# Layer 0 of a two-layer transformer block: values meet exponentials in two steps of a job instead of four

## The chip, the cores and the metric

The kernel runs on one core of one Trainium2 chip. The metric is the device time of one launch in microseconds (us). It was run three times before the change: 2089.46, 2091.49 and 2093.51 us, so the median is 2091.49 us.

The core has five engines with a queue of their own each: PE (matrix products; its weight loads are shown apart, as PEld), DVE (vector), ACT (activation functions), POOL and SP (here SP only issues DMAs). PE writes to PSUM, which this kernel takes as eight banks of 128 partitions by 512 fp32 values. All data is fp32.

## The reference

Eight sequences of 512 tokens with 256 features go through two layers. In each, a normalized input goes into an attention branch and a feed-forward branch, and both are added to the residual. The change is in layer 0:

```python
x = L0_attn_x                                   # (8, 512, 256)
xn = _layernorm(x)
# attention, 16 heads of 16 features, no mask, no scale
qkv = (xn @ W_qkv + b_qkv).reshape(B, D, 3, H, p).transpose(2, 0, 3, 1, 4)
q, k, v = qkv
scores = softmax(einsum('bhip,bhjp->bhij', q, k))
attn = einsum('bhij,bhjp->bhip', scores, v)
# experts: each token goes to the one of 8 experts that its affinity picks
es = argmax(xn @ centroids.T); alpha = sigmoid(max(xn @ centroids.T))
ffn = alpha * (xn + relu(ln(xn) @ w1[es].T + b1[es]) @ w2[es].T + b2[es]) + (1 - alpha) * xn
x = x + attn + ffn
```

Layer 1 then runs two causal attentions with a convolution between them, and a low-rank feed-forward branch. The change does not touch its code.

## The kernel before

**Jobs and steps.** Layer 0's attention is cut into 32 jobs: sequence b (8) by group g of four heads (4). A job is worked in 8 steps for the row maxima (`Job.scores`) and, 12 steps later (`LEAD[0]`), in 8 steps for the exponentials (`Job.exps`). Between the two, `Job.shift` turns the maxima round on PE (L375), copies them (L380, DVE) and puts them by four small DMAs into a spare row of the queries (L382, SP), so that the second product comes out already shifted. `run` (L442) walks over the steps. One step t does the following on PE, in this order:

- the scores: two heads of maxima (L345) and two heads of exponents (L394), four products of 32 rows each that run side by side on the four strips of 32 rows of PE. A step's exponents are of one block of 128 keys (`kc`) and one pair of heads (`SC_SEQ[0]`), so a block of keys is complete after two steps;
- the filling (`work_of.fill`, L488): other work of layer 0 by due times and costs, such as projections (L293), values (L303), the expert branch (`Block`: L785, L807, L828). It comes in pieces, so that some steps get none;
- the attends (`attend`, L489 and L427): for the blocks of keys that `AV_AT[0]` (L85) lists for this step, `Job.attend` multiplies exponentials by values (L434): four heads, each on its own 32 columns of PE, into the one bank of `av`.

DVE follows the scores with two maxima (L362), ACT with two exponentials (L421). In the text, step i of a job means the step with its exponents i = 0 to 7; an attend listed at 8 falls into step 0 of the next job. After the last block, `l0_done` (L901) transposes the result on DVE (L904), divides (L906, L908) and adds on POOL (L912).

**Banks.** The maxima take turns on a ring `mx`, the exponents on a ring `sc`: three banks each (`banks_alone`), but two each while the experts run (`banks_experts`, L218). After the last maxima, `sc` has five (`banks_last`) and one turn of the loop does two steps of exponents.

**Experts.** The normalized tokens are scattered by expert into two DRAM arrays `hs_d` (L749), which were filled with zeros before (L866, two DMAs on SP). Then 23 blocks of 256 tokens follow. `Block(n+1)` is made right after the first quarter of block n's hidden layer: it gathers its weights (`w`, L764, POOL's queue), loads its tokens from both arrays into `hs0` and `hs1` (L773, SP) and adds them on POOL (L778). `features` transposes them on PE (L785) after the last quarter of block n. `output` adds the bias on DVE into `f` (L837) and SP stores `f` (L839). `hs0`, `hs1` and `f` have one buffer each.

**Order.** The kernel writes out the order of every engine's queue itself (`manual_schedule`, L156); the framework only adds semaphores.

## Time and profile before

| What | us |
|---|---|
| median of three runs | 2091.49 |
| profiled execution, its own time | 2091.93 |
| its span on the core | 2090.0 |
| PE busy | 2001.5 (96%) |
| DVE busy | 1230.1 (59%) |
| ACT busy | 867.6 (42%) |
| POOL busy | 203.4 (10%) |

The stages, as the trace lays them out:

| us from the span's start | stage |
|---|---|
| 0 to 70 | norms, first maxima, affinities; zeros go to DRAM from 10.56 on |
| 70 to 180 | attention of layer 0 with routing and scatters, little filling |
| 180 to 928 | attention with the experts as filling |
| 928 to 989 | the last jobs, gathers, second norm |
| 989 to 1112 | layer 1's feed-forward branch |
| 1112 to 2090 | layer 1's attentions |

PE's busy share counts matmuls that are pipelined and whose ends are modelled, so 96% does not mean that nothing is lost. What a piece costs PE is better read from starts: from the first instruction of one group to the first of the next. In the timeline, each line is a run of like instructions: start, duration, engine, line, operation, out<-in, shapes, count, and in brackets the idle time before it with what ended it. An fp32 product shows as two instructions.

### The profile page before, as it was taken

How to read it: one execution, taken by the hardware profiler on the slowest of the kernel's cores; microseconds unless marked ns; L12 is line 12 of the kernel's file. 1: busy time of each engine (PE TensorE's matmuls, PEld its weight loads, DVE VectorE, ACT ScalarE, POOL GpSimd, SP SyncE). 2: the span in 40 equal slices, each digit the busy share in tenths (PEclk: the TensorE clock that was granted, in tenths of full speed). 3: DMA queues.
4: the chain of work that ended last, by engine and by line, in shares of the span. 5: the costliest groups of instructions: out<-in, count | busy, mean ns of one | idle time of the engine just before them, and what ended most of it. 6: DMA issues, size and time to landing. Idle time of an engine off the chain costs nothing.

```text
span 2090.0 us, 35594 instructions
## 1 busy us (share of the span) xinstructions
PE 2001.5 (96%) x13672; PEld 1013.6 (48%) x13672; DVE 1230.1 (59%) x3565; ACT 867.6 (42%) x1690; POOL 203.4 (10%) x245
## 2 busy tenths in 40 slices
PE   5899999999999999998898999999999999999998
PEld 3334555555555555542334455554555555554554
DVE  5765555555455455565425666666666666666763
ACT  4444333333333333346541444444444444444444
POOL 4361010010110100013310000000000000000000
PEclk8899999999999999999997899999999999999999
DMA  9015132222322122202000000000000000000000
GB/s 329 25 64 184 59 117 81 94 79 96 117 78 97 67 108 107 74 26 80 21 0 1 2 2 2 2 12 2 2 13 2 12 2 12 2 12 2 2 12 21
DMA packets 46058, 105.60 MB, mean 51 GB/s; under 512 B 5953, under 2 KB 33985, under 8 KB 42945
## 3 DMA queue, kind: packets, MB, share of 16 engines
q0 software_dynamic: 6384, 59.78, 7.7%
q1 hardware_dynamic: 38656, 42.62, 6.1%
q8 instruction: 107, 1.75, 0.4%
q10 hardware_dynamic: 848, 0.93, 0.1%
q14 instruction: 63, 0.51, 0.1%
HBM read 76.05 MB, written 26.48 MB: 49 GB/s over the span
## 4 chain that ended last, share of the span: by engine, by line
PE 87%; DVE 6%; ACT 2%; issue 2%; DMA 1%; SPq 0%; POOL 0%; ACTq 0%; DVEq 0%; POOLq 0%
PE bank L345 30%; PE bank L434 13%; PE bank L828 8%; PE bank L807 8%; PE bank L293 5%; PE bank L412 4%; PE bank L1085 4%; PE bank L394 3%; PE bank L303 3%; PE bank L1103 2%; DVE m L362 2%; PE bank L990 1%; PE bank L1137 1%; PE bank L266 1%; PE bank L1003 1%
## 5 line engine op out<-in xcount | busy, mean ns | idle before, releaser
L421 ACT ACTIVATE e<-bank 128x512 f32<-128x512 f32 (+1 forms) x1280 | 639.1, 552 | 919.5 <-PE bank L394 460.4
L345 PE MATMUL bank<-k,q 32*128 32x512 f32 (+3 forms) x3072 | 761.0, 534 | 22.2 <-DVE m L362 18.3
L394 PE MATMUL bank<-q,k 32*128 32x512 f32 (+3 forms) x3072 | 681.2, 533 | 4.5 <-DMA q<-mT 3.4
L365 DVE CUSTOM_DVE_ANT_0 jk<-bank,cmask 128x512 bf16<-128x512 f32 (+3 forms) x1024 | 502.9, 491 | 240.8 <-PE bank L345 162.4
L345 PEld LDWEIGHTS bank<-k,q 32*128 32x128 f32 x3072 | 301.2, 186 | 384.1 <-issue 162.1
L362 DVE TENSOR_REDUCE m<-bank 128x1 f32<-128x512 f32 x512 | 328.9, 685 | 142.8 <-PE bank L394 111.8
L434 PE MATMUL bank<-e,v 128*32 128x512 f32 (+3 forms) x3072 | 317.4, 501 | 0.0
L394 PEld LDWEIGHTS bank<-q,k 32*128 32x128 f32 x3072 | 266.2, 186 | 15.0 <-issue 9.6
L807 PE MATMUL bank<-hsT,w 128*128 128x256 f32 x736 | 179.6, 389 | 1.3 <-DVE hsT L790 1.3
L828 PE MATMUL bank<-w,hT 128*128 128x256 f32 x736 | 170.9, 386 | 0.0
L807 PEld LDWEIGHTS bank<-hsT,w 128*128 128x128 f32 x736 | 133.3, 190 | 69.9 <-issue 52.8
L828 PEld LDWEIGHTS bank<-w,hT 128*128 128x128 f32 x736 | 137.4, 191 | 38.1 <-issue 21.0
L434 PEld LDWEIGHTS bank<-e,v 128*32 128x32 f32 x3072 | 67.5, 108 | 137.1 <-issue 132.0
L412 PE MATMUL bank<-mask_t,ident_bf 128*128 128x128 bf16 (+1 forms) x768 | 123.5, 244 | 0.0
L412 PEld LDWEIGHTS <-ident_bf 128*128 128x128 bf16 x768 | 44.0, 97 | 155.5 <-issue 140.5
L820 DVE TENSOR_SCALAR hT<-bank,w 128x256 f32<-128x256 f32 x92 | 44.5, 484 | 110.3 <-ACT hT L818 110.3
L1085 PE MATMUL bank<-ctxT,cw_sb 128*128 128x256 f32 x384 | 90.0, 383 | 2.1 <-DVE q L283 1.8
L365 DVE DVE_READ_ACCUMULATOR2_ANT m<- 128x1 f32 x1024 | 85.0, 83 | 0.0
L837 DVE TENSOR_TENSOR f<-bank,w 128x256 f32<-128x256 f32 x46 | 19.5, 425 | 104.2 <-PE bank L828 104.1
L285 ACT ACTIVATE k<-bank,bqk,rows 128x512 f32<-128x512 f32 x64 | 46.3, 773 | 73.8 <-PE bank L293 64.5
L818 ACT ACTIVATE hT<-bank,w 128x256 f32<-128x256 f32 x92 | 43.6, 474 | 79.8 <-PE bank L807 79.8
L1085 PEld LDWEIGHTS bank<-ctxT,cw_sb 128*128 128x128 f32 x384 | 70.1, 189 | 13.2 <-DVE q L283 3.2
(187 smaller groups left out, 1410.5 us busy)
## 6 DMA issues: line engine op xcount, KB each, us to landing
hs_d<-zeros SPq DMA_DIRECT2D x2, 5888.0 KB
hs<-hs_d SPq DMA_DIRECT2D x46, 256.0 KB
q<-mT SPq DMA_DIRECT2D x384, 2.0 KB
fs_d<-f SPq DMA_DIRECT2D x23, 256.0 KB
acc<-in_x SPq DMA_DIRECT2D x8, 512.0 KB
out<-acc SPq DMA_DIRECT2D x8, 512.0 KB
cw_sb<-in_conv_w SPq DMA_DIRECT2D x1, 768.0 KB
wqk<-in_a_wqk ACTq DMA_DIRECT2D x1, 512.0 KB
```

The costliest lines, as they stand in the source:

```text
L293: nc.tensor.matmul(ps, lhsT=w[:, k, col : col + P], rhs=src[:, k, :], start=(k == 0), stop=(k == 1))
L303: nc.tensor.matmul(ps[:, j * D : (j + 1) * D], lhsT=src[:, k, c * P : (c + 1) * P], rhs=w[:, k, :], start=(k == 0), stop=(k == 1),)
L345: lambda h=h, qc=qc, at=at, nk=nk: nc.tensor.matmul(heads[h % 2][:, at : at + nk], lhsT=self.q[h * PH : (h + 1) * PH, qc * P : (qc + 1) * ...
L362: nc.vector.tensor_reduce(self.m[:, qc, h, :], src, AX.X, ALU.max, negate=True)
L365: nc.vector.tensor_tensor_reduce(out=junk[:, :nk], in0=src, in1=cmask[:, S - nk :], scale=1.0, scalar=-3e38, op0=ALU.add, op1=ALU.max, acc ...
L394: lambda h=h, kc=kc, at=at, lo=lo: nc.tensor.matmul(heads[h % 2][:, at : at + S - lo], lhsT=self.k[h * PH : (h + 1) * PH, kc * P : (kc + 1 ...
L412: nc.tensor.matmul(heads[h][:, : len(blocks) * P], lhsT=ident_bf, rhs=mask_t[:, : len(blocks) * P], start=False, stop=True,)
L421: nc.scalar.activation(e[:, h, :], heads[h][:, :n], AF.Exp, scale=self.scale)
L434: nc.tensor.matmul(self.av[h * PH : (h + 1) * PH, lo:], lhsT=self.v[:, kc, 4 * self.g + h, :], rhs=es[h // 2][:, h % 2, :], start=first, s ...
L807: nc.tensor.matmul(ps[:, i * TB : (i + 1) * TB], lhsT=w[:, O_W1 + k * FF + fc * P : O_W1 + k * FF + (fc + 1) * P], rhs=self.hsT[:, k, :], ...
L828: nc.tensor.matmul(ps[:, 0:D], lhsT=self.hT[:, fc, j * P : (j + 1) * P], rhs=w[:, O_W2 + fc * D : O_W2 + (fc + 1) * D], start=(fc == 0), s ...
L1085: nc.tensor.matmul(ps[:, :w], lhsT=cw_sb[:, k, tap, c * P : (c + 1) * P], rhs=ctxT[b % 2][:, k, tap + lo : tap + lo + w], start=(k == 0 an ...
```

## The change

Layer 0's attends are listed for two steps of a job, two blocks each, instead of for four steps with one block each. Exponentials of up to four steps then wait for their values, so their ring gets a fifth tile (128 partitions of 4 KB). Its memory comes from two places: the tile of zeros is halved (the two DMAs that clear `hs_d` now write rows of 1 KB instead of 2 KB, as many bytes), and `hs1` shares the buffer of `f`.

```diff
 AV_AT = (
-    {2: (0,), 4: (1,), 6: (2,), 8: (3,)}, {5: (0,), 6: (1, 3), 7: (2,)}, {2: (0,), 4: (1, 3), 6: (2,)},
+    {4: (0, 1), 8: (2, 3)}, {5: (0,), 6: (1, 3), 7: (2,)}, {2: (0,), 4: (1, 3), 6: (2,)},
 )
...
                 e = self.pool.tile(
                     [P, 2, n], F32, tag=f"e{blocks[0]}" if self.causal else "e", name=f"e{self.nm}_{i}",
-                    bufs=3 if self.causal else 4,
+                    bufs=3 if self.causal else 5,
                 )
...
-        zeros = pre.tile([P, 2 * D], F32, name="zeros")
+        zeros = pre.tile([P, D], F32, name="zeros")
         nc.gpsimd.memset(zeros, 0.0)
-        hs_z = [h.rearrange("(n p r) d -> p n (r d)", p=P, r=2) for h in hs_d]
+        hs_z = [h.rearrange("(n p) d -> p n d", p=P) for h in hs_d]
...
-                    hs = moe.tile([P, TB // P, D], F32, tag=f"hs{i}", name=f"hs{n}_{i}", bufs=1)
+                    hs = moe.tile([P, TB // P, D], F32, tag=("hs", "f")[i], name=f"hs{n}_{i}", bufs=1)
...
-                        nc.sync.dma_start(out=h, in_=zeros.unsqueeze(1).to_broadcast([P, NBLK, 2 * D]))
+                        nc.sync.dma_start(out=h, in_=zeros.unsqueeze(1).to_broadcast([P, NBLK * TB // P, D]))
```

In the built programs every engine has as many instructions as before. On PE only the attends stand in other places: those listed for 2 and 6 have moved to 4 and 8, behind the same step's filling. The other queues keep their order; what is new there are two waits: each `hs1` load (SP) also waits until an earlier store of `f` has landed, and each first write of `f` (DVE) also waits for POOL's sum of the next block's tokens.

## The prediction

> **What bounds the kernel now.** I read the page first: the busy shares and the shares of the chain of waits by line.

> ```profile
> PE 2001.5 (96%) x13672; PEld 1013.6 (48%) x13672; DVE 1230.1 (59%) x3565; ACT 867.6 (42%) x1690; POOL 203.4 (10%) x245
> PE 87%; DVE 6%; ACT 2%; issue 2%; DMA 1%; SPq 0%; POOL 0%; ACTq 0%; DVEq 0%; POOLq 0%
> ```

> PE sets the end, so the question is what PE gets through, stage by stage. The windows by stage (PE, PEld, DVE, ACT, POOL busy, granted clock, DMA share, GB/s):

> ```profile
> 70.00:180.00 110.00, 99.27 (x537) 34.88 (x536) 73.41 (x144) 47.99 (x88) 57.51 (x72) 0.95 0.29 100
> 180.00:928.00 748.00, 735.37 (x4051) 393.93 (x4050) 391.00 (x706) 266.93 (x496) 65.37 (x67) 1.00 0.24 87
> 928.00:989.00 61.00, 51.64 (x295) 17.22 (x292) 39.18 (x94) 39.26 (x74) 25.69 (x27) 0.94 0.29 86
> ```

> Layer 0 is PE's in the expert stage, less so before and after it. Then PE's timeline, close up. First in the expert stage:

> ```profile
> 883.83 1.07 PE L434 MATMUL bank<-e,v 128*32 128x512 f32 x8
> 884.82 0.70 PE L345 MATMUL bank<-k,q 32*128 32x512 f32 x2
> 884.84 0.70 PE L394 MATMUL bank<-q,k 32*128 32x512 f32 x2
> ...
> 886.73 1.29 PE L345 MATMUL bank<-k,q 32*128 32x512 f32 x3 [0.76 <-DVE m L362]
> 887.33 0.70 PE L394 MATMUL bank<-q,k 32*128 32x512 f32 x2
> ...
> 888.39 1.99 PE L303 MATMUL bank<-wv,xT 128*128 128x256 f32 x8
> 890.32 1.06 PE L434 MATMUL bank<-e,v 128*32 128x512 f32 x8
> 891.31 0.70 PE L345 MATMUL bank<-k,q 32*128 32x512 f32 x2
> ```

> Starts give PE's price list: an attend of one block 0.99 (883.83 to 884.82, 890.32 to 891.31), the scores 1.07 (887.33 to 888.39), eight filling products 1.93. But the step at 884.84 has neither filling nor attend, and the next one's exponents start only at 887.33, 2.49 later: PE waits for DVE's maxima to free the banks. I call a step without filling bare. Then the same stretch before the experts, with three banks a ring:

> ```profile
> 142.15 1.06 PE L434 MATMUL bank<-e,v 128*32 128x512 f32 x8
> 143.16 0.70 PE L394 MATMUL bank<-q,k 32*128 32x512 f32 x2
> 145.06 0.70 PE L394 MATMUL bank<-q,k 32*128 32x512 f32 x2
> 146.12 1.06 PE L434 MATMUL bank<-e,v 128*32 128x512 f32 x8
> ```

> A bare step lasts 1.90 here (143.16 to 145.06), and 2.07 with an attend (1.07 + 0.99).

> **What a merge saves.** Layer 1 shows attends of other widths:

> ```profile
> 1502.33 0.64 PE L434 MATMUL bank<-e,v 128*32 128x256 f32 x8
> 1502.90 0.48 PE L345 MATMUL bank<-k,q 32*128 32x256 f32 x2
> ...
> 1514.58 1.07 PE L434 MATMUL bank<-e,v 128*32 128x384 f32 x16
> 1515.58 0.59 PE L345 MATMUL bank<-k,q 32*128 32x384 f32 x2
> ```

> 256 columns take 0.57; two blocks in one go (384 + 128 columns, 16 instructions) take 1.00, as much as one block of 512. So an attend is 0.143 once plus 0.853 per 512 columns (1.00 = a + b, 0.57 = a + b/2). Two blocks together: 1.85 instead of 1.99. There are 64 merges (32 jobs, two each): 64 x 0.142 = 9.1 us, if PE pays for every attend.

> [...]

> **The sum, step by step.** I listed from PE's timeline, for the steps of layer 0, what stands between one group of L394 and the next. Steps i = 2 and 6 of a job lose an attend, i = 0 and 4 double theirs.

> *Expert stage (steps 40 to 230 of 256).* Losing: 48 steps. 36 have filling and get 0.995 shorter: -35.8. 12 are bare: these last 2.50 with an attend (857.53 to 860.02) as without one (2.49 above), so they save 0. Doubling: 48 steps. 42 have filling: +0.853 each, +35.8. 6 are bare: from 2.50 to 1.07 + 1.85 = 2.92, +0.42 each, +2.5. Sum +2.5. Filling without an attend (1.07 + 1.93 = 3.00) stays above 2.50, so no new wait arises.

> *Two blocks of experts whose tokens come late.*

> ```profile
> 679.20 1.26 POOL L778 TENSOR_TENSOR hs<-hs,hs 128x512 f32<-128x512 f32 x1 [15.62 <-DMA hs<-hs_d]
> 680.52 0.42 PEld L785 LDWEIGHTS bank<-ident,hs 128*128 128x128 f32 x4 [1.62 <-POOL hs L778]
> ```

> PE waits for block 16's tokens; for block 18 POOL's sum ends at 745.57 and PE's transposes start at 745.63. Both loads follow, on SP's queue, a shift in a step 5; the transposes are in the step 7 after it. Step 6 between them loses its attend, PE comes 1.0 earlier and waits as much longer. So 1.0 of the saving is lost twice: +2.0 (0 to 3).

> *Before the experts (steps 4 to 39, nine half jobs).* Nearly all bare. Four steps last 2.07 + 1.90 + 2.07 + 1.90 = 7.94. Afterwards 2.92 + 1.90 + x + y, where x and y are bare steps that follow a bare step; the trace has none with three banks. Lower end 1.20 each: DVE's maxima start 0.60 apart (144.31, 144.91, 145.51), two a step. Upper end 1.90 as now. So 7.22 to 8.62, -0.72 to +0.68 a half job. Between them: ACT's exponential starts 1.24 after its product (143.16 to 144.39) and takes 0.60, so a product that comes 1.20 after the last one finds its second bank free only at 1.90; its strip is then held for 0.86 to 2.76. That makes x 1.20, y 1.56 and some 0.5 carried into the doubled step: 8.08, +0.15. Times nine: +1.4 (-6.5 to +6.1).

> *Steps 232 to 243.* DVE is busy all of 934 to 944 (2.00 of each 2 us), so attends there cost nothing now. Of the doubled ones, the two in a step 0 are covered by `l0_done` on DVE (1.4: 932.47 to 934.01 and its like), the third is not wholly: +0.5 (0 to 2.5).

> *End of layer 0.* PE mostly waits for ACT. The last attend (987.65 to 988.65) becomes double, with layer 1's first product right behind it: +0.85 (0 to 1.7).

> *Fifth tile.* The exponentials of step i + 5 take the tile of step i, which the attend of step i + 4 at the latest has read; on PE this stands before the scores that step i + 5 waits for anyway: 0. The bank `av` has four steps of rest instead of two: 0, as no wait for it shows now.

> *Zeros.* As many bytes in rows half as long. 2 x 5888 KB went at 408 GB/s (25 to 40 us); the loads of `acc`, with rows of 1 KB, at 349 (5 to 15 us). So 34.5 instead of 29.6 us: the end moves from about 47 to 52. Next on SP's queue is the first shift at 64.97, the scatters start at 83.58: hidden, 0. Without that cover it would cost 5.

> *`hs1` in `f`'s buffer.* `hs1` waits for the store of the block before the current one. The nearest row for its landing: POOL's first gather waits for the last store, issued at 926.50, and starts at 929.55, so 3.05 at most. In eleven blocks the store is issued 0.5 before the loads (395.90, 396.36), so `hs1` starts up to 2.1 later. Behind it on SP stand shifts, needed three steps on. POOL's sum ends 6.2 or more before PE's transposes in these eleven. Worst case: the load falls among the weights' 2.2 MB, as for block 1, where POOL's sum starts 12.35 after the weights' issue (169.27 to 181.62). For block 14 that gives 595.12 + 12.35 + 1.27 = 608.74, against transposes at 608.88; blocks 5, 7, 12, 17 are alike. They just make it: 0; if not, about 1 each, +5. DVE's `f` waits for POOL's sum of the next block: 680.47 against 685.93, long done.

> Sum: 2.5 + 2.0 + 1.4 + 0.5 + 0.85 = +7.3. The profiled span of 2090.0 becomes 2097.3; around it lie 1.9 (2091.93 - 2090.0), and that run is 0.4 above the median of the three, so I put it onto the median: 2091.5 + 7.3 = 2098.8.

> **The rivals.**
> - *Every attend is paid (faster).* The merges save their 9.1, and bare steps give room elsewhere: 2082.4. For it: the widths in layer 1, PE at 96%. Against it: the bare steps, which last as long without an attend.
> - *Bare steps in a row run at DVE's pace (no change).* x = y = 1.20 before the experts: 7.3 - 1.4 - 6.5 = -0.6, 2090.9. For it: DVE is 67% busy there (73.41 of 110). Against it: the exponents' banks.
> - *Bare steps keep their 1.90 (slower still).* +6.1 instead of +1.4: 2103.5. It decides as soon as x + y exceeds 3.5. For it: it is the only length the trace shows.

> **How the numbers follow.** Forecast 0.58 (its own range 2094 to 2103), every attend paid 0.12, DVE's pace 0.15, 1.90 kept 0.15. Two tenths of a per cent, about what a measurement can tell, are 4.2 us: below 2087.3 is faster, above 2095.7 slower. Faster: the first rival and a little, 0.13. Same: the second, and the forecast's low end, 0.10, together 0.25. Slower: 0.62. The lows of the parts reach the second rival, the highs, with late `hs1`, 2106; the low end is put to 2086 for a part of the first rival.

> **What would show it.** In the profile after: attends of 16 instructions taking 1.85; bare steps 2 and 6 in the expert stage still 2.50 long; the wait of L785 for POOL longer by 1.0 at blocks 16 and 18; steps 2 and 3 before the experts near 1.2 and 1.6; `hs_d<-zeros` landed before 60 us. The prediction is wrong if bare steps shrink with their attend taken away, if two blocks cost other than 1.85, or if L785 waits in more blocks.

## The result and the profile after

| | before | after |
|---|---|---|
| median (us) | 2089.40 (6 runs, 2088.76 to 2093.51) | 2111.07 (6 runs, 2105.05 to 2113.64) |
| profiled execution, its own time | 2091.93 | 2105.97 |
| its span | 2090.0 | 2104.1 |

The changed kernel is slower: ratio 1.0093, 95% interval 1.008 to 1.0107. Two later sets of runs of it gave 1.0072 and 1.0089. The direction was foreseen. The size was not: +7.3 us was predicted, and the measured time lies above the predicted range. The medians are 21.7 us apart. The profiled execution of the kernel after is one of its two fastest, 5.1 below its median, and shows +14.2 us; so some 7 us of that difference show in no profile of this pair. The stretches of the profiled execution say where the 14.2 are. The marks are the starts of the first exponents (L394) of a step, of L978 and of layer 1's first maxima:

| stretch | before | after | difference | predicted |
|---|---|---|---|---|
| start to step 4 | 86.16 | 83.77 | -2.39 | 0 |
| steps 4 to 39 | 94.41 | 100.51 | +6.10 | +1.4 |
| steps 40 to 230 (experts) | 747.88 | 750.76 | +2.88 | +2.5 + 2.0 |
| steps 231 to 247 | 36.87 | 39.19 | +2.32 | +0.5 |
| step 248 to the first L978 | 23.33 | 26.56 | +3.23 | +0.85 |
| feed-forward of layer 1 | 120.61 | 122.26 | +1.65 | 0 |
| attentions of layer 1 | 980.69 | 981.09 | +0.40 | 0 |

The page of the kernel after, its busy times and the shares of its chain of waits:

```profile
PE 2000.3 (95%) x13672; PEld 1023.9 (49%) x13672; DVE 1230.2 (58%) x3565; ACT 868.3 (41%) x1690; POOL 204.6 (10%) x245
PE 87%; DVE 7%; ACT 3%; issue 2%; DMA 1%; POOL 0%; SPq 0%; ACTq 0%; DVEq 0%; POOLq 0%
```

PE is busy for 1.2 us less than before, and the span is 14 longer, so PE waits longer. It also works more slowly in places, as the windows by stage of the kernel after show (PE, PEld, DVE, ACT, POOL busy, granted clock, DMA share, GB/s). The granted clock is the share of PE's full clock that it was given; 0.50 is half clock.

```profile
70.00:184.00 114.00, 100.81 (x520) 41.42 (x519) 71.24 (x140) 46.87 (x85) 57.69 (x73) 0.93 0.28 98
184.00:935.00 751.00, 727.45 (x4052) 396.06 (x4050) 391.40 (x706) 267.30 (x496) 65.13 (x67) 1.00 0.24 86
935.00:1001.00 66.00, 55.42 (x299) 19.33 (x298) 38.43 (x93) 39.40 (x73) 27.14 (x27) 0.90 0.26 78
```

Against 0.95, 1.00 and 0.94 before, the granted clock is lower in the two stages where time was lost beyond the prediction: before and after the experts. First PE's timeline of the kernel after in the expert stage, to be laid beside the same steps of before:

```profile
891.28 0.70 PE L394 MATMUL bank<-q,k 32*128 32x512 f32 x2
...
893.77 0.70 PE L394 MATMUL bank<-q,k 32*128 32x512 f32 x2
...
894.83 1.99 PE L303 MATMUL bank<-wv,xT 128*128 128x256 f32 x8
896.76 1.92 PE L434 MATMUL bank<-e,v 128*32 128x512 f32 x16
898.61 0.70 PE L345 MATMUL bank<-k,q 32*128 32x512 f32 x2
```

Two blocks in one go take 1.85 (896.76 to 898.61); the bare step still lasts 2.49 (891.28 to 893.77). Then step 4, which has the first doubled attend. Before the change it ran at full clock (1.00 from 86.16 to 94.00):

```profile
86.16 0.70 PE L394 MATMUL bank<-q,k 32*128 32x512 f32 x2
...
87.22 1.07 PE L434 MATMUL bank<-e,v 128*32 128x512 f32 x8
88.22 0.70 PE L345 MATMUL bank<-k,q 32*128 32x512 f32 x2
```

And in the kernel after:

```profile
80.60 0.69 PE L345 MATMUL bank<-k,q 32*128 32x512 f32 x1 [2.23 <-DVE m L362]
...
83.77 1.22 PE L394 MATMUL bank<-q,k 32*128 32x512 f32 x2
...
85.78 3.20 PE L434 MATMUL bank<-e,v 128*32 128x512 f32 x16
88.90 0.70 PE L345 MATMUL bank<-k,q 32*128 32x512 f32 x2
```

A doubled attend, the same 16 instructions as above, takes 3.12 here (85.78 to 88.90) instead of 1.85, and the scores ahead of it 2.01 instead of 1.07. Behind step 38 it is the same with the first experts' products; the first line is of the kernel before, the second of the kernel after:

```profile
175.21 5.42 PE L807 MATMUL bank<-hsT,w 128*128 128x256 f32 x24 [1.27 <-DVE hsT L790]
```

```profile
177.34 7.00 PE L807 MATMUL bank<-hsT,w 128*128 128x256 f32 x24 [1.62 <-DVE hsT L790]
```

The windows around the two places in the kernel after (columns as above):

```profile
78.20:81.60 3.40, 1.17 (x9) 0.52 (x8) 3.23 (x9) 0.60 (x1) 0.42 (x1) 1.00 0.01 2
81.60:88.40 6.80, 6.51 (x27) 1.40 (x23) 3.82 (x8) 2.17 (x4) 6.10 (x8) 0.50 0.18 61
173.70:177.10 3.40, 2.02 (x12) 0.85 (x10) 2.08 (x4) 1.84 (x4) 0.00 (x0) 1.00 1.00 426
177.10:180.50 3.40, 3.16 (x8) 2.56 (x9) 0.59 (x2) 0.00 (x0) 0.00 (x0) 0.51 1.00 422
```

In the 3.4 us before (as long as the shorter of the two stretches at half clock), PE was busy for 1.17 and 2.02, with longest single gaps of 2.23 and 1.62; after that it was granted half its clock (0.50 and 0.51) for 6.8 and 3.4 us. An attend stood in both places before the change (steps 2 and 38). This gave the theory for the experiments: the prediction's prices are right, and what it lacks is that an attend in a place where PE waits anyway is not only free, it also keeps the clock up.

### The profile page after: what moved, and what is told of

It is laid out like the page before. It is cut to its first block, busy times and chain, and to the rows that moved or that the text cites. A ratio compares the mean times of both kernels' runs of the same rounds, so it can differ in the third digit from the quotient of the medians.

```text
span 2104.1 us, 35591 instructions
## 1 busy us (share of the span) xinstructions
PE 2000.3 (95%) x13672; PEld 1023.9 (49%) x13672; DVE 1230.2 (58%) x3565; ACT 868.3 (41%) x1690; POOL 204.6 (10%) x245
## 4 chain that ended last, share of the span: by engine, by line
PE 87%; DVE 7%; ACT 3%; issue 2%; DMA 1%; POOL 0%; SPq 0%; ACTq 0%; DVEq 0%; POOLq 0%
PE bank L345 29%; PE bank L434 13%; PE bank L807 8%; PE bank L828 8%; PE bank L293 5%; PE bank L1085 4%; PE bank L412 4%; PE bank L394 3%; PE bank L303 3%; DVE m L362 2%; PE bank L1103 2%; PE bank L266 1%; PE bank L1137 1%; PE bank L990 1%; PE bank L1003 1%
## 5 line engine op out<-in xcount | busy, mean ns | idle before, releaser
L345 PE MATMUL bank<-k,q 32*128 32x512 f32 (+3 forms) x3072 | 761.8, 533 | 32.4 <-DVE m L362 28.4
L394 PE MATMUL bank<-q,k 32*128 32x512 f32 (+3 forms) x3072 | 688.2, 534 | 4.2 <-DMA q<-mT 3.1
L345 PEld LDWEIGHTS bank<-k,q 32*128 32x128 f32 x3072 | 302.5, 186 | 370.8 <-issue 157.9
L362 DVE TENSOR_REDUCE m<-bank 128x1 f32<-128x512 f32 x512 | 328.8, 685 | 121.3 <-PE bank L394 94.7
L434 PE MATMUL bank<-e,v 128*32 128x512 f32 (+3 forms) x3072 | 305.0, 500 | 0.0
L394 PEld LDWEIGHTS bank<-q,k 32*128 32x128 f32 x3072 | 270.3, 186 | 18.4 <-ACT e L421 8.7
L434 PEld LDWEIGHTS bank<-e,v 128*32 128x32 f32 x3072 | 74.4, 109 | 146.9 <-issue 142.2
```

What stands on the lines that cost most here:

```text
L345: lambda h=h, qc=qc, at=at, nk=nk: nc.tensor.matmul(heads[h % 2][:, at : at + nk], lhsT=self.q[h * PH : (h + 1) * PH, qc * P : (qc + 1) * ...
L362: nc.vector.tensor_reduce(self.m[:, qc, h, :], src, AX.X, ALU.max, negate=True)
L394: lambda h=h, kc=kc, at=at, lo=lo: nc.tensor.matmul(heads[h % 2][:, at : at + S - lo], lhsT=self.k[h * PH : (h + 1) * PH, kc * P : (kc + 1 ...
L434: nc.tensor.matmul(self.av[h * PH : (h + 1) * PH, lo:], lhsT=self.v[:, kc, 4 * self.g + h, :], rhs=es[h // 2][:, h % 2, :], start=first, s ...
```

## The experiments

All of them are compared with runs of the kernel before on the same chip. On the chips of e9/e10 and e11/e12 that kernel itself took 2098.3 and 2102.0, elsewhere 2089.4 to 2091.7, so times of different chips are not set against each other. In the profiles the difference lies mainly in steps 231 to 247: they take 45.73 in e10 and 38.24 in e5, which is the same program, and 49.54 in e12 and 39.19 in the kernel after. Why was not looked into. In kernels with added lines, the same code stands up to five lines further down.

### The memory edits alone (e1)

```diff
 # before, with zeros in rows of 1 KB and hs1 in the buffer of f; four tiles
```

> The kernel before with the change's memory edits alone: zeros in rows of 1 KB, hs1 in f's buffer; four tiles and four attends a job as before. Theory (the loss is what the attends no longer hide, plus lost clock where PE waits longer): 0, within 2 us of before. Rival (the memory edits delay the experts' tokens or the scatters): most of the loss of 15 to 20 us, 2100 or more.

Measured: 2089.61 against 2091.70, ratio 0.9981 (0.9965 to 0.9997). The two edits cost nothing. In the kernel after the longer way of `hs1` shows, but stays hidden: for block 14 POOL's sum runs from 613.44 to 614.71, 10.7 after the weights' issue at 602.72 instead of 3.7 as before, and PE's transposes start at 616.34.

### One merge at a time (e2, e3, e4)

```diff
-    {4: (0, 1), 8: (2, 3)},
+    {4: (0, 1), 6: (2,), 8: (3,)},     # e2
+    {2: (0,), 4: (1,), 8: (2, 3)},     # e3
```

e4 is the kernel after, unchanged, on the same chip.

> The kernel after with attends {4: (0, 1), 6: (2,), 8: (3,)}: one merge a job, the one in step 4. By the list of steps: expert stage 18 filled steps 2 lose 0.995 (-17.9), 6 bare ones lose nothing, 19 filled steps 4 gain 0.853 (+16.2), 5 bare ones 0.42 (+2.1): +0.4; the rest near 0. Theory: +0 to +3 us. Rival (each merge costs the same, or memory costs): +8 to +20.

> The kernel after with attends {2: (0,), 4: (1,), 8: (2, 3)}: one merge a job, the one in the next job's step 0. By the list: expert stage 18 filled steps 6 lose 0.995 (-17.9) of which 2.0 comes back as waits for blocks 16 and 18, 6 bare ones lose nothing, 23 filled steps 0 gain 0.853 (+19.6), one bare one 0.43: +4.1; before the experts +0.7, end of layer 0 +0.85 and 0.5: about +6, and on top whatever clock is lost at the end of layer 0. Theory: +6 to +14 us, nearly all of the change's loss. Rival (each merge costs the same): half of the loss, +8 to +10; if memory costs: +15 or more.

> The kernel after, unchanged, for another profile beside the others. Theory: 2104 to 2113 us; the price of each step the same as in the first profile (step 4 before the experts 3.2, filled steps as listed), and what differs from run to run is where the granted clock is 0.5. Rival (the spread comes from DMAs): steps of the expert stage differ between the profiles.

Measured: e2 2092.48, ratio 1.0008 (0.999 to 1.0025); e3 2102.01, 1.0058 (1.0041 to 1.0076); e4 2107.31, 1.0072 (1.0051 to 1.0093). Step 4 of e4 took 5.12, at half clock again, and not the 3.2 expected. By the times, most of the loss comes with the second merge, which empties steps 6: step 38 and the steps ahead of the two late blocks among them. By the stretches the two are nearer. Steps 4 to 39 take 97.6 in e2 and 97.5 in e3, against 94.4 before and 100.5 after. Each merge has its place there: e2 has the half clock in step 4, behind the empty step 2, and e3 has it in step 39, behind the empty step 38. Steps 40 to 230 take 747.3 and 752.6 (747.9 before), step 231 to the first L978 62.6 and 65.3 (60.2 before). For e2 these sum to +5.0, where its median shows +0.8; its profile has layer 1's attentions 7.8 shorter than that of before. The programs do not differ there, and that stage takes 973 to 982 us in the sixteen profiles; why it varies was not settled.

### Old places at the ends only (e6)

```diff
-            av_at = AV_AT[job.seq]
+            av_at = OLD if layer == 0 and j in (0, 4, 29, 30, 31) else AV_AT[job.seq]
```

`OLD` is the list of before; the other 27 jobs have the merges.

> The kernel after, with attends in four steps again in jobs 0, 4, 29, 30 and 31 alone, that is at the start of the exponentials, ahead of the experts and at the end of layer 0. Theory: these three places make most of what the sum by steps missed; step 4 falls from 5.15 to 2.07, step 39 from 10.73 to about 8.4, the end of layer 0 comes within 1 us of that of before relative to step 231; what is left is the expert stage's +3 to +6: 2094 to 2099 us. Rival (the loss is spread evenly over the merges): 27 of 32 jobs are still merged, so 0.84 of the loss: 2105 or more.

Measured: 2096.02 against 2090.04, ratio 1.0033 (1.0018 to 1.0049). Five jobs of 32 undone take back more than half of the loss: step 231 to the first L978 lasts 60.03 (60.20 before, 65.75 after), step 39 8.39 (8.35 and 10.73).

### What a bare step holds (e5, e7, e9, e10)

e5 is the kernel before, with 14 attends put off by one step, from a filled step into the bare step behind it; four tiles, no merge.

```diff
+LATER = (50, 52, 76, 90, 108, 134, 136, 150, 152, 162, 176, 178, 194, 218)
...
-                attends.setdefault(lead + steps * j + i, []).append(...)
+                at = steps * j + i
+                if layer == 0 and at in LATER:
+                    at += 1
+                attends.setdefault(lead + at, []).append(...)
```

> The kernel before (four tiles, four attends a job, no memory edit) with 14 attends put off by one step, from a filled step of the expert stage into the bare step after it. Theory (an attend in a bare step of that stage is free): the filled steps get 0.99 shorter, the bare ones stay at 2.50: -14 us, about 2077. Rival (PE pays for every attend wherever it stands): 0, within 2 us of before.

Measured: 2074.78 against 2090.04, ratio 0.9933 (0.9913 to 0.9954): faster than both kernels, by about what was expected. PE's timeline of e5, the step that the prediction quoted as bare (884.84 before):

```profile
866.42 0.70 PE L397 MATMUL bank<-q,k 32*128 32x512 f32 x2
...
867.47 1.06 PE L437 MATMUL bank<-e,v 128*32 128x512 f32 x8
868.47 1.13 PE L348 MATMUL bank<-k,q 32*128 32x512 f32 x2
868.91 0.70 PE L397 MATMUL bank<-q,k 32*128 32x512 f32 x2
```

It has an attend now and lasts 2.49, as without one. The 14 steps that gave theirs away are 0.99 to 1.00 shorter each. (Step 178 is 2.68 shorter: the profile of before had a granted clock of 0.50 from 723.10 to 726.50 there.)

e7 is the kernel before with a third bank for the maxima, taken from the filling.

```diff
-        share_banks(mx=banks[:2], sc=banks[4:6], av=banks[6:7], mm=banks[2:4] + banks[7:])
+        share_banks(mx=banks[:3], sc=banks[4:6], av=banks[6:7], mm=banks[3:4] + banks[7:])
```

> The kernel before with three banks for the maxima in the expert stage, and two instead of three for projections, values and experts. Theory (a bare step lasts 2.50 there because two banks wait for DVE's maxima): bare steps fall to 1.9 to 2.1, 32 of them: -10 to -14 us, less what the filling loses by its third bank. Rival (bare steps wait for the exponentials): bare steps stay at 2.4 or more; time 0 or worse.

Measured: 2086.38 against 2090.04, ratio 0.9985 (0.9971 to 0.9998), less than expected. PE's timeline of e7, a step that took 2.50 before (857.53 to 860.02):

```profile
852.65 0.70 PE L394 MATMUL bank<-q,k 32*128 32x512 f32 x2
...
853.71 1.07 PE L434 MATMUL bank<-e,v 128*32 128x512 f32 x8
...
854.72 0.99 PE L394 MATMUL bank<-q,k 32*128 32x512 f32 x2
```

It takes 2.07, the PE work alone. Bare steps without an attend go from 2.50 to 1.90. So the banks of the maxima set the 2.50. All 32 bare steps together are 15.7 shorter than before; the filled ones, with two banks instead of three for the filling, are 10.1 longer, and that is why little is left.

e9 is e5 with a fifth tile (and the memory edits for it) and 7 further attends put off by two steps, into bare steps that have one already. e10 is e5 again, on the same chip.

```diff
+MERGE = (68, 82, 100, 116, 140, 210, 226)
...
+                    at += 1 if at in LATER else 2 if at in MERGE else 0
```

> The kernel before, with the 14 attends of the cover experiment put off by one step into bare steps of the expert stage, and 7 further attends put off by two steps, into a bare step that has one attend already (so that this step has two blocks in a row, as in the change), with the change's memory edits for the fifth tile. My theory (an attend in a bare step is free, two of them make it 2.92 instead of 2.50, and an attend taken out of a filled step saves 0.995): the 14 give what the cover experiment gave (about -15 us against the kernel before), the 7 give 7 x (0.995 - 0.42) = -4 more: -19, about 2071. Rival (PE must not be idle at all: the saving is given back, by a lower granted clock or by later waits): -15 or less, 2075 or more. Second rival (the fifth tile or the waits of the memory edits cost something once the stage is shorter): above 2078.

> The cover experiment once more, on the same chip as the one with 7 merges, for their difference: about 2075. By my theory it stands 4 us above the other, by the rivals level with it or below it.

Measured: e9 2079.83, ratio 0.9917 (0.9893 to 0.994); e10 2082.49, 0.9921 (0.99 to 0.9942). The times alone do not tell the two apart. The profiles do, in the expert stage: against e10 the bare steps are 3.01 longer (7 x 0.43) and the filled ones 6.86 shorter (7 x 0.98), together -3.9 where -4 was expected. So merging pays where the attend leaves a filled step for a bare one.

### Unread work in the idle places (e8, e11, e12)

e8 is the kernel after with one product behind steps 2 and 38, which nothing reads.

```diff
+            if layer == 0 and t - lead in (2, 38):
+                nc.tensor.matmul(bank(), lhsT=ident, rhs=xT[0][:, 0, :], start=True, stop=True)
             attend(t)
```

> The kernel after, with one product of 128 rows by 512 columns that nobody reads added behind steps 2 and 38, where an attend was taken away: work is added, nothing moved. Theory (there PE idles so long without the attend that the granted clock is 0.5 in the steps that follow): the clock stays or returns to 1.0, step 4 falls from 5.15 to 3.2 and step 39 from 10.7 to about 8.5: 3 to 5 us faster than after. Rival (the steps are long for another reason): 0 to 2 us slower than after.

Measured: 2104.21 against 2090.04, ratio 1.0075 (1.0055 to 1.0096). That is not apart from e4's 1.0072 on the same chip; the time alone decides nothing. PE's timeline of e8, step 4 and the first experts' products:

```profile
84.77 0.70 PE L394 MATMUL bank<-q,k 32*128 32x512 f32 x2
...
85.83 1.93 PE L434 MATMUL bank<-e,v 128*32 128x512 f32 x16
87.68 0.70 PE L345 MATMUL bank<-k,q 32*128 32x512 f32 x2
...
176.34 5.42 PE L809 MATMUL bank<-hsT,w 128*128 128x256 f32 x24 [1.32 <-DVE hsT L792]
```

Step 4 takes 2.92 instead of 5.15, step 39 8.39 instead of 10.73: 4.6 us that were half clock and nothing else, since the instructions of these steps are the same (granted 1.00 from 177.10 to 180.50 in e8, 0.51 in the kernel after). Not all of it is a gain: step 40 starts 2.6 us earlier than in the kernel after (181.70 instead of 184.28), as the start of step 4 is 1.0 later and step 38 is 0.8 longer.

All sixteen profiles (before, after and the fourteen runs) agree. In four of them (after, e2, e4, e12) step 2 has nothing but its scores, and in these four step 4 has 4.6 to 5.1 us of half clock; in the twelve others it has none. In four (after, e3, e4, e12) step 38 has nothing but its scores, and in these four step 39 has 3.4 us of half clock; in the twelve others it has none.

e11 was meant to do this at the end of layer 0 too, with two more products ahead of the transposes of sequences 5 and 7. e12 is the kernel after, on the same chip.

```diff
         ps = bank()
+        if nm in ("c5", "c7") and k == 0:
+            for _ in range(2):
+                nc.tensor.matmul(ps, lhsT=ident, rhs=xT1[0][:, 0, :], start=True, stop=True)
```

> The kernel after, with one unread product of 512 columns behind steps 2 and 38, and two such products ahead of the transposes (L266) of the tokens of sequences 5 and 7 at the end of layer 0, where PE otherwise waits 2.3 us for ACT's normalized tokens; nothing reads the products. Theory of the granted clock (PE idle for a few us, then half the clock for 3.4 or 6.8 us, in which a doubled attend takes 2.6 instead of 1.9): the windows at half clock from 983 on are gone, the attends and scores behind them are back at 1.92 and 1.14, and the stretch from step 231 to the first L978 is 3 us shorter than the 65.7 of the kernel after; with the 2.6 at step 39 the whole is 5 to 7 us faster than the kernel after. Rival (only the cover that the attends gave to the wait for ACT is lost, the clock does not matter): 65 to 67 us as before, the whole at most 3 us faster than after.

> The kernel after, unchanged, on the same chip as the one with four places filled by unread products, for their difference: 1.007 to 1.011 of the kernel before; 65 to 67 us from step 231 to the first L978.

Measured: e11 2116.45, ratio 1.0063 (1.0047 to 1.0079); e12 2121.27, 1.0089 (1.0073 to 1.0104). The products missed their place: sequences 5 and 7 are transposed in layer 1, where they ran at 1069 and 1093. So e11 tells nothing of layer 0's end; it is e8 once more, and beside e12 it is 4.8 us faster. From step 231 to the first L978 e12 took 75.5 us, not the 65 to 67 expected; this is where its chip is slower.

### The end of layer 0 (e13, e14)

e13 has the two pairs ahead of the transposes of sequences 1 and 3, e14 is e8 again on the same chip.

```diff
-        if nm in ("c5", "c7") and k == 0:
+        if nm in ("c1", "c3") and k == 0:
```

> The kernel after, with one unread product of 512 columns behind steps 2 and 38, and two such products ahead of the transposes (L266) of the tokens of sequences 1 and 3, where PE otherwise waits 2.3 us for ACT's normalized tokens at the end of layer 0; nothing reads the products. Theory of the granted clock: the windows at half clock that fall on the last two attends are gone, these attends are back from 2.6 to 1.92 and the scores ahead of them from 2.09 to 1.14, and the stretch from the last wait for the shifted queries to the first L978 is 2 to 3 us shorter than in the kernel without the pairs on the same chip. Rival (only cover is lost, ACT sets the pace): the attends stay at 2.6 or the stretch stays within 0.5 us.

> The kernel after, with one unread product behind steps 2 and 38 only, on the same chip as the one with two pairs more: 3 to 5 us faster than the kernel after (1.005 to 1.008 of the kernel before); half clock on one or two of the last three attends (2.6 instead of 1.92).

Measured: e13 2097.94 against 2090.25, ratio 1.0043 (1.0028 to 1.0059); e14 2104.81, 1.0075 (1.0051 to 1.0099). By the medians the unread work in two more places saves 6.9 us; the profiles show how much of this is its doing. PE's timeline of e14, without the pairs:

```profile
981.54 1.81 PE L266 MATMUL bank<-ident,yn 128*128 128x128 f32 x6 [2.28 <-ACT yn L257]
983.29 2.09 PE L394 MATMUL bank<-q,k 32*128 32x512 f32 x8
985.31 2.82 PE L434 MATMUL bank<-e,v 128*32 128x512 f32 x16
...
995.58 2.81 PE L434 MATMUL bank<-e,v 128*32 128x512 f32 x16
998.32 1.98 PE L980 MATMUL bank<-yT,u_sb 128*128 128x512 f32 x4
```

And of e13, with them (L267 is the unread work):

```profile
978.91 1.99 PE L267 MATMUL bank<-yT,ident 128*128 128x512 f32 x4 [0.35 <-DVE yT L271]
...
982.87 1.14 PE L397 MATMUL bank<-q,k 32*128 32x512 f32 x8
983.94 1.92 PE L437 MATMUL bank<-e,v 128*32 128x512 f32 x16
...
992.78 1.92 PE L437 MATMUL bank<-e,v 128*32 128x512 f32 x16
994.64 1.98 PE L983 MATMUL bank<-yT,u_sb 128*128 128x512 f32 x4
```

The wait of 2.28 is filled, the attends take 1.92 instead of 2.8, the scores 1.14 instead of 2.09. The granted clock says the same; the first window is e14's, the second e13's:

```profile
980.40:987.20 6.80, 5.64 (x26) 2.21 (x30) 0.69 (x1) 4.22 (x9) 0.00 (x0) 0.50 0.00 0
```

```profile
980.30:987.10 6.80, 5.53 (x37) 2.01 (x35) 0.69 (x1) 6.34 (x14) 0.00 (x0) 1.00 0.00 0
```

From step 248 to the first L978 it is 23.02 instead of 26.84. This is 3.8 of the 7.6 us between the two spans. Another 3.6 lies in layer 1's attentions (977.45 and 981.10), where the programs do not differ; that stage takes 973 to 982 in the profiles, longest where a stretch of 20.5 us at half clock falls at its start instead of 6.8 us, and is not counted for the pairs.

## Why the prediction was right in direction and wrong in size

*Expert stage, +2.5, and late blocks, +2.0: right.* Bare steps that lost their attend stayed at 2.50, filled ones became 1.00 shorter, doubled ones 0.86 longer, bare doubled ones 2.92. Step 167 (4.87 to 5.76) and step 183 (5.26 to 6.33) gave the saving back to the tokens of blocks 16 and 18; the kernel after, PE's weight load ahead of its first transpose of block 16:

```profile
687.26 0.42 PEld L785 LDWEIGHTS bank<-ident,hs 128*128 128x128 f32 x4 [2.51 <-POOL hs L778]
```

1.62 became 2.51. The stage's +2.88 includes step 178, which lost 2.68, 1.68 more than its attend, to the half clock that, of these two profiles, only the one of before has there: 2.88 + 1.68 = 4.6, for 4.5 predicted. The profile of e4 shows two such stretches in this stage (from 689 and 733), with +6.4 against before. One of them follows the longer wait for block 16's tokens. So a late block may have cost more than the 1.0 predicted there, and part of what the medians show beyond the profile may lie here; that was not separated.

*Before the experts, +1.4: the term that failed, measured +6.1.* Its bare steps x and y were right. The first exponents of steps 24 to 27 of the kernel after start at

```profile
137.54 0.70 PE L394 MATMUL bank<-q,k 32*128 32x512 f32 x2
...
140.47 0.70 PE L394 MATMUL bank<-q,k 32*128 32x512 f32 x2
...
142.79 0.70 PE L394 MATMUL bank<-q,k 32*128 32x512 f32 x2
...
143.98 0.69 PE L394 MATMUL bank<-q,k 32*128 32x512 f32 x1
```

and step 28 at 145.56: 2.93, 2.32, 1.19, 1.58, where 1.20 and 1.56 had been put for x and y. That the four make 8.02, for the predicted 8.08, is luck: the 2.32 had been put at 1.90, and these four steps lasted 8.36 before the change, not 7.94. Nor did each half job become 0.15 longer. Apart from the half clock, half jobs that begin with a step 0 became 0.3 to 0.5 shorter, and those that begin with a step 4 became 0.2 to 0.9 longer. Of the 6.1, 4.6 is the half clock in steps 4 and 39 (e8), and 1.5 is left, near the predicted 1.4 as the balance of the two. The step that failed is that the work behind the emptied steps 2 and 38 was priced at full clock: the lost clock, 4.6 us, had no term. The rival in which bare steps keep their 1.90 also gives 6.1, but by another way: they did not keep it.

*Steps 232 to 243, +0.5: measured +1.6, within its bounds (0 to 2.5).* Step 232 went from 2.22 to 3.30, step 239 from 2.31 to 3.10. Steps 244 to 247 add 0.9, for which there was no term: the doubled attend of step 245 ran at half clock (2.66 instead of 1.92; granted 0.50 from 965.60 to 969.00). How much of the 2.3 of the whole stretch is clock was not separated; half clock stood there in e13 and e14 too.

*End of layer 0, +0.85: failed, measured +3.2.* The last attend and layer 1's first product, in the kernel before and in the kernel after:

```profile
987.65 1.06 PE L434 MATMUL bank<-e,v 128*32 128x512 f32 x8
988.65 1.98 PE L978 MATMUL bank<-yT,u_sb 128*128 128x512 f32 x4
```

```profile
998.18 2.68 PE L434 MATMUL bank<-e,v 128*32 128x512 f32 x16
1000.79 1.55 PE L978 MATMUL bank<-yT,u_sb 128*128 128x512 f32 x3
```

The doubled attend costs 2.61 instead of 1.00, as it runs at half clock (0.51 from 996.30 to 999.70), and so does the one before it (0.50 from 982.70 to 989.50). In e13, at full clock (1.00 from 990.50 to 997.30), the last one takes 1.86 (992.78 to 994.64): the +0.86 of the prediction. So the second half of the last attend is paid as predicted. What failed is again the price of the work behind the waits, which the prediction put at full clock. Half clock as such is not new in this stretch: 6.8 us of it lie in the 23.33 us of the kernel before and 10.2 in the 26.56 of the kernel after. In e13, which has none, the stretch takes 23.02. That it is 0.3 shorter than before the change is therefore not the merge's doing; whether unread work would also have helped the kernel before was not tried.

*Fifth tile, zeros, `hs1`, 0 each: right.* e1 shows it for the last two; the fifth tile has no run of its own, but e9, which has it, gained in the expert stage what was expected. The transfers run at 385 GB/s from 20 to 40 us (408 before) and are at rest from 50 on (from some 47 before; 52 was predicted), long ahead of the first scatter at 81.2.

*Every attend paid* fell with the bare steps: e5 gained by moving attends into them. As an estimate from several runs, the sum without the half clock that was found would be 4.6 (experts) + 1.5 + 2.3 + 0.9 = 9.3 for the predicted 7.3, with whatever half clock lies in the 2.3. The time of e13, in which steps 2 and 38 and the waits at the end are filled, is near that, 1.0043 or +9 us (6 to 12), although it includes the unread products. What the prediction lacked was one price: what the work behind a wait costs when the wait is no longer filled.

Two entries of the table are not the change's. The first 86 us differ by 2.4 with the half clock of the first steps (0.53 from 74 to 85 in the kernel before, 0.57 from 71 to 79 and 0.50 from 81.60 in the kernel after), and e1, without any merge, has 84.11 there. So step 40 starts 3.7 later in the kernel after than in this profile of before, and 5.6 later than in e1. The feed-forward stage's 1.65 goes with half clock (0.51 from 1044.20 to 1047.60); e1 has the like at 1031.

## What to carry to other kernels

Price every matmul by the step it stands in. Here a bare step, whose length the banks of the maxima set, lasted 2.49 with an attend as without one, and a filled step that gave its attend away became 0.99 to 1.00 shorter; moving 14 attends from filled steps into bare ones gained 0.7% (e5). Before taking work out of a wait, add up PE's busy time over the surrounding few us, not only the wait: here half clock followed 3.4 us in which PE was busy for 34% and for 59%, and did not follow others with 46% and 52%. Where such a place can't be filled with real work, an unread product can be tried: with two pairs of them the end of layer 0 took 23.02 in e13, without them 26.84 in e14.

## What the runs showed of the hardware

Bare steps of the expert stage (1.07 of work in 2.50, 2.07 with an attend) mostly did not cost the clock: from 180 to 928 of the kernel before, with 32 of them, the granted clock was 1.00, and half clock followed once. Ahead of 723.10, with bare step 177 in it, PE was busy for 2.21 of 3.40 us, and the next 3.4 us, in step 178, ran at 0.50.

Nor does idle time explain every such stretch: in layer 1, from 1139 of the kernel before, 20.5 us ran at half clock (0.50 from 1139.50 to 1160.00) although PE had been busy for 3.10 of the 3.4 us before. What brings that, and whether it can be avoided, was not tried.
